# Global attention and a convolutional layer in one kernel: the values of 29 blocks as seven block products each

## The chip, the core and the metric

The kernel runs on one core of a Trainium2 chip. The metric is the device time of one execution in microseconds (us), the median of several runs. The core has five engines with queues of their own: TensorE (PE in the profile; its weight loads are shown apart as PEld), VectorE (DVE), ScalarE (ACT), GpSimd (POOL) and SyncE (SP), which here issues most DMA transfers. [...] All data is float32. Each float32 matmul of the kernel shows as two instructions in the trace.

## What is computed

The input is four images of 64 x 64 pixels with 256 channels. The first layer is global self-attention, and the second a perception convolution, a two-layer network on each pixel, and local 3 x 3 attention. Cut to what matters:

```python
# layer 0, per image: N = 4096 pixels, C = 256 channels
q = x @ Wq + bq                      # 32 columns
k = x @ Wk + bk
v = x @ Wv + bv                      # 256 x 256: the part that is changed
attn = softmax(q @ k.T)
x = gamma * (attn @ v) + x
# layer 1
perceived = depthwise_3x3(x, w_perc) # 3 outputs per channel
hid = gelu(perceived @ w_up1 + b_up1)
h = x + hid @ w_up2 + b_up2
out = h + local_attention_3x3(h, w_qkv, b_qkv)
```

## The kernel before

**Blocks and slots.** An image is cut into 8 blocks of 512 pixels (8 rows). Four images give 32 blocks, and the main loop has one slot for each: `for slot in range(NSLOT)`. In slot s, the global attention of block s runs against all pixels of its image. Behind it, with fixed lags, run the layers that follow, for earlier blocks: the convolution of block s-2 (`perceive`), the network of block s-3 (`hidden_part`, `update_part`, `guide_part`) and the local attention of block s-5.

**Points.** A slot has 16 points, `point = 2 * G + half`, where G is the key block of 512 pixels and half its first or second 256 pixels. At an even point `energy` makes the scores of the next key block (4 PSUM banks, tile e); at every point `weight` takes their exponentials on ScalarE (tile p), the jobs in `jobs[point]` follow, then `product` adds values times weights into two banks (tile acc), and `add_up` adds the weights on VectorE for the denominator (tile den). Then VectorE gets as many steps of the convolution as `share[point]` says: 6, 7, 7, 5, 4, 3, 3, 3, 2, 2, 4, 5, 5, 4, 0, 0. A step is a tap of 512 elements (line 477) or a mix of two quarters of 256 (line 483). At a slot's end `partial_sums` and `finish` divide the sums, add to the pixels, and release acc. All this is a schedule written by hand (`tc.manual_schedule`): the program order is each engine's queue order, and the framework adds the waits that data and buffers require.

**Banks.** PSUM is held by e (4 banks, one buffer), acc (2) and tag "m" (2 buffers). Every other product of the main loop, `job_bank(name)` or `bank("m", name)`, takes the next "m" bank in turn, and waits until the use before last of it has been read out.

**Values.** `project_v(s, pair)` makes the values of 256 pixels of block s: two tiles of 128 pixels, each two matmuls (256 input channels in two halves) of 256 columns, into one bank, and one ScalarE copy into tile v. `staged[s]` (tile xc and others) holds the block's pixels, channels on partitions, in two channel halves; `project_qk(s)` makes queries and keys of blocks s and s+1 out of them. Tile v has 8 buffers, one image. Blocks 0 to 2 are done ahead of the loop and blocks 3 to 7 in slot 0 (`early_jobs`). The values of the next image, in slots 7, 15 and 23 (`g == NBLK - 1`), come in `nxt[G]` behind the product and the convolution steps of each odd point: both halves of one block, and at every other one a `project_qk`. `fetch` loads the pixels two blocks ahead.

**Seven products.** Other products of the kernel are already made as seven block products instead of eight (Winograd's form of Strassen's algorithm): `hidden_part`, `update_part`, `guide_part`. `mix_weights` on GpSimd makes four mixes t1 to t4 of a weight's four blocks, VectorE makes mixes of the moving side, the products are called a to g and come in the parts "ab", "cd", "eg", "f", and `gather` puts each part's sums together: one ScalarE copy and one VectorE sum for ab, two sums for cd, three for eg, one for f. A part is read out by the sums that stand in VectorE's queue at that place. In `update_part` and `guide_part` the parts stand in points of their own, or two parts in one point.

Of the kernel before, what the change touches and what calls it, by code (L numbers as in the profile page):

```python
# [9 lines left out]
F32 = mybir.dt.float32  # L10
AF = mybir.ActivationFunctionType
ALU = mybir.AluOpType
# [40 lines left out]
def attention_then_perception_kernel(  # L53
# [37 lines left out]
    def unshifted():  # L91
# [184 lines left out]
                values[s][:, 2 * pair : 2 * pair + 2, :], ps.rearrange("p (t c) -> p t c", c=C)  # L276
            )

        def projections(s):
            pair = [lambda: project_qk(s)] if s % 2 == 0 else []  # L280
            return [lambda: project_v(s, 0), lambda: project_v(s, 1)] + pair

        def spread_queries(s):

# [227 lines left out]
        lower = by_turns(range(NPC), range(LOW, TAPS), RB - 1, RB)  # L512


        wmix = pool.tile([P, 4, MULT, C], F32, tag="wmix", name="wmix")


        wmix2 = pool.tile([P, 3, CH, P], F32, tag="wmix2", name="wmix2")
# [2 lines left out]
        def mix_weights(y11, y12, y21, y22, t1, t2, t3, t4):  # L521
            for to, a, b in ((t1, y12, y11), (t2, y22, t1), (t3, y22, y12), (t4, y21, t2)):
                nc.gpsimd.tensor_tensor(to, a, b, ALU.subtract)
# [42 lines left out]
        def hidden_part(s, d, part):  # L566


            if d == 0 and part == 0:
                hids[s] = tile_of([P, NHC, NB], "hid", f"hid_{s}")  # L570

            q = hids[s].rearrange("p d (a n) -> p (d a) n", a=2)
            q11, q21, q12, q22 = 2 * d, 2 * d + 1, 2 * d + 4, 2 * d + 5
            y11, y21 = (lambda j, u=u: wup1[:, u + j, bass.ts(d, P)] for u in (0, MULT))
            y22 = lambda j: wup1[:, MULT + j, bass.ts(d + 2, P)]
            t1, t2, t3, t4 = (lambda j, i=i: wmix[:, i, j, bass.ts(d, P)] for i in range(4))

            def products(name, *todo):
                ps = job_bank(f"hid_{s}_{d}_{name}")
                for n, (w, kind) in enumerate(todo):  # L580
                    for j in range(MULT):
                        nc.tensor.matmul(  # L582
                            ps[:, n * C : (n + 1) * C], lhsT=w(j), rhs=mixes[s, j][:, kind, :],
                            start=(j == 0), stop=(j == MULT - 1),
                        )
                return ps.rearrange("p (a n) -> p a n", a=2)

            def add(to, a, b):
                nc.vector.tensor_tensor(to, a, b, ALU.add)  # L589

            def twice(t):
                return t.unsqueeze(1).to_broadcast([P, 2, C])

            if part == 0:
                nc.scalar.copy(q[:, q22, :], products("a", (y11, LOWER))[:, 0, :])
                bc = products("bc", (y21, UPPER), (t2, MIX2))
                add(q[:, q11 : q22 + 1 : q22 - q11, :], bc, twice(q[:, q22, :]))
            else:
                de = products("de", (t3, MIX3), (t1, MIX1))
                both = q[:, q21 : q12 + 1 : q12 - q21, :]  # L600
                add(both, de, twice(q[:, q22, :]))
                add(q[:, q22, :], q[:, q21, :], de[:, 1, :])
                add(both, products("gf", (t4, UPPER2), (y22, MIX4)), both)
                for i in (d, d + 2):
                    nc.scalar.activation(  # L605
                        hids[s][:, i, :], hids[s][:, i, :], AF.Gelu, bias=bup1[:, i : i + 1]
                    )
# [411 lines left out]
        def local_product(s, c, behind=None):  # L1019
# [30 lines left out]
            nc.vector.tensor_tensor(rv, ov, pixels(s, c), ALU.add)  # L1050
            nc.sync.dma_start(out=out[b, :, c, bass.ts(g, NB)], in_=res)

        def job(f, s, *args, n=NSLOT):
            return [lambda: f(s, *args)] if 0 <= s < n else []

# [24 lines left out]
        def early(s):  # L1080
            fetch(s)
            fetch(s + 1)
            project_qk(s)

        early_jobs = [lambda: early(4), *projections(3), lambda: early(6)]
        early_jobs += [*projections(4)[:2], *projections(5), *projections(6)[:2], *projections(7)]
        points = 2 * NG
        for slot in range(NSLOT):
            b, g = divmod(slot, NBLK)
            if slot >= RING:  # L1090
# [13 lines left out]
            ]  # L1104
            if slot in (1, 2):
                jobs[0] = [lambda: next(combine)] * 2
            nxt = []
            if g == NBLK - 1 and b + 1 < B:
                nxt = [projections(slot + 1 + i) for i in range(NBLK)]
                for i in range(2):  # L1110
                    fetch(slot + 1 + i)
            if slot == 0:
                nxt = [early_jobs[2 * i : 2 * i + 2] for i in range(NG)]
            conv = perceive(slot - LAG_PERC, mixed) if slot >= LAG_PERC else iter(())
            n_mixed = NPC * (TAPS - 1) + MULT * len(MIXED)
            n_steps, stepped = n_mixed, 0
# [3 lines left out]
            if slot == NSLOT - 1:  # L1120

                nc.sync.dma_start(out=wup2[:, :CH, P:], in_=w_up2[:, :CH, P:])


                jobs = [
                    job(hidden_part, k, 0, 0) + job(local_values, k - 1, 1),
                    job(local_denominator, a) + job(hidden_part, k, 0, 1),
                    job(hidden_part, k, 1, 0), job(hidden_part, k, 1, 1) + job(local_product, a, 0),
                    job(update, k, 0), job(update, k, 1) + job(local_product, a, 1),
                    job(guide, k, 0) + job(local_values, k, 0),  # L1130
                    job(guide, k, 1) + job(local_values, k, 1),
                    job(scores, k, 0) + job(hidden_part, k + 1, 0, 0),
                    job(scores, k, 1) + job(local_sum, k - 1) + job(hidden_part, k + 1, 0, 1),
                    job(hidden_part, k + 1, 1, 0) + job(local_total, a + 1)
                    + job(local_reciprocal, a + 1),
                    job(hidden_part, k + 1, 1, 1), job(update, k + 1, 0) + job(border, k),
                    job(local_product, a + 1, 0) + job(update, k + 1, 1),
                    job(local_product, a + 1, 1) + job(local_values, k + 1, 0),
                    job(local_values, k + 1, 1),
                ]  # L1140
                conv = chain(conv, perceive(slot - 1, upper))
                n_steps += NPC * (TAPS - 1)
            for point in range(points):
                G, half = divmod(point, 2)
                after = slot + (G + 1) // NG, (G + 1) % NG
                if half == 0:
                    if G == NG // 2 and slot + 1 < NSLOT:
                        spread_queries(slot + 1)
                    if after[0] < NSLOT:
                        energy(*after)  # L1150
                if after[0] < NSLOT:
                    weight(*after, half)
                for do in jobs[point]:
                    do()
                product(slot, G, half)

                if point == 0:
                    add_up(slot, 0, 0)
                if point < points - 1:
                    add_up(slot, *divmod(point + 1, 2))  # L1160
                else:
                    partial_sums(slot)


                if slot < NSLOT - 1:
                    to = sum(share[: point + 1])
                else:
                    to = min(n_steps, -(-(point + 1) * n_steps // (points - 2)))
                    if point < 3:
                        to = min(to, n_mixed // MULT)  # L1170
                while stepped < to:
                    next(conv, None)
                    stepped += 1
                if slot == 0 and point == NG:

                    next(combine)
                    blqk = loaded(b_lqk, "blqk")
                    wperc = loaded(w_perc, "wperc")
                    bperc = loaded(b_perc, "bperc")
                    wup1 = loaded(w_up1, "wup1")  # L1180
                    bup1 = loaded(b_up1, "bup1")
                    wup2 = loaded(w_up2, "wup2")
                    mix_weights(
                        *blocks_of(wup1, MULT, C), *(wmix[:, i] for i in range(4))
                    )
                    y = blocks_of(wup2, CH, P)
                    mix_weights(*y, wmix2[:, 0], wmix2[:, 1], y[1], wmix2[:, 2])
                    bup2 = loaded(b_up2, "bup2")
                    nc.sync.dma_start(out=wlv, in_=w_qkv[:, :, 2 * C :])
                    blv = loaded(b_lv.partition_broadcast(P), "blv", [P, C])  # L1190
                if nxt and half == 1:
                    for do in nxt[G]:
                        do()
                    if slot and G + 2 < NBLK:
                        fetch(slot + 1 + G + 2)
            for _ in conv:
                pass
            if slot < NSLOT - 1:
# [467 lines left out]
```

## Time and profile before

| | |
|---|---|
| median of 3 runs | 3459.62 us (3457.77 to 3460.63) |
| profiled span | 3455.9 us |
| TensorE clock granted | 0.999 |
| slot 7 / slot 8 | 137.15 us / 102.05 us |
| values, line 270 | 512 matmul instructions, 116.3 us of TensorE |
| copies of values, line 275 | 64 on ScalarE, 586 ns each |
| attention product, line 323 | 4096 instructions, 1835.0 us of TensorE |

A line of the profile's groups reads: source line, engine, operation, output <- inputs, shapes and count | busy time in us, mean ns of one | idle time of the engine just before, and what ended it. Matmuls are pipelined, so the mean of one is longer than the step from one to the next; busy time counts overlaps once. The chain of waits is the chain of work that ended last, followed back from the end; where it stays on one engine without gaps, that engine's work is the time.

### The profile page before, as it was taken

Reading aid. Unit: us, or ns where it says so; the run is one execution under the profiler, and the core shown is the slowest. Engines: PE = TensorE matmul, PEld = TensorE weight load, DVE = VectorE, ACT = ScalarE, POOL = GpSimd, SP = SyncE. Lnnn points to the kernel's source line nnn. Section 1 sums busy time; section 2 is a strip of 40 time slices with the busy share of each in tenths; the row PEclk is TensorE's granted clock in tenths of the full one; section 3 lists DMA queues with packets and bytes.
Section 4 is the critical chain, followed back from the end, with each engine's and each line's share of the span. In section 5 each row is a group of like instructions: output and inputs, shape, how many; then the busy total and the mean of one; then the engine's idle time right before and its main releaser. Section 6 shows DMA issues by size and latency. Waiting matters only on the chain.

```text
span 3455.9 us, 33709 instructions
## 1 busy us (share of the span) xinstructions
PE 3442.0 (100%) x12726; PEld 1995.0 (58%) x12726; DVE 2736.2 (79%) x4439; ACT 1063.8 (31%) x1328; POOL 355.7 (10%) x525
## 2 busy tenths in 40 slices
PE   9999999999999999999999999999999999999998
PEld 5445555556555556556555555566656555555555
DVE  2388888767888888875888888887688888888885
ACT  3233333323332233333333323333233333223331
POOL 2000001110111110111001111101110011111021
PEclk9999999999999999999999999999999999999999
DMA  4000000120000000011000000001100000000000
GB/s 107 7 4 10 7 10 16 28 48 17 16 15 8 16 16 16 22 28 43 16 10 16 10 13 16 16 22 30 41 16 16 16 10 7 16 16 18 7 7 26
DMA packets 93274, 67.05 MB, mean 19 GB/s; under 512 B 65872, under 2 KB 71248, under 8 KB 92976
## 3 DMA queue, kind: packets, MB, share of 16 engines
q1 hardware_dynamic: 92432, 64.42, 6.9%
q8 instruction: 102, 1.67, 0.2%
q14 instruction: 68, 0.56, 0.1%
q10 hardware_dynamic: 672, 0.39, 0.0%
HBM read 43.62 MB, written 18.81 MB: 18 GB/s over the span
## 4 chain that ended last, share of the span: by engine, by line
PE 98%; DVE 1%; DMA 0%; SPq 0%; ACT 0%; issue 0%; ACTq 0%; POOL 0%; DVEq 0%
PE acc L323 51%; PE e L304 8%; PE hid_de L582 4%; PE hid_gf L582 4%; PE hid_bc L582 4%; PE v L270 3%; PE lv L891 3%; PE lo L1025 3%; PE s L932 3%; PE hid_a L582 3%; PE dx_ab L534 2%; PE dx_cd L534 1%; PE dx_eg L534 1%; PE hid L614 1%; PE g_cd L534 1%; PE qk L236 1%
## 5 line engine op out<-in xcount | busy, mean ns | idle before, releaser
L323 PE MATMUL acc<-p,v 128*128 128x512 f32 x4096 | 1835.0, 594 | 0.3 <-DVE o L388 0.3
L323 PEld LDWEIGHTS acc<-p,v 128*128 128x128 f32 x4096 | 768.0, 190 | 809.9 <-issue 793.0
L477 DVE SCALAR_TENSOR_TENSOR perc<-xp,wperc,perc 128x512 f32<-128x512 f32 (+2 forms) x1554 | 1101.2, 770 | 32.4 <-ACT perc L473 32.2
L312 ACT ACTIVATE p<-e 128x1024 f32<-128x1024 f32 x512 | 524.0, 1024 | 1717.5 <-PE e L304 713.3
L337 DVE TENSOR_TENSOR den<-den,p 128x1024 f32<-128x1024 f32 x480 | 586.4, 1222 | 86.5 <-ACT p L312 84.7
L957 POOL TENSOR_TENSOR lp<-lp,near 128x396 f32<-128x396 f32 x60 | 96.4, 1607 | 2490.8 <-ACT lp L952 2490.8
L304 PE MATMUL e<-qa,ka 32*128 32x512 f32 x2048 | 291.9, 640 | 0.0
L304 PEld LDWEIGHTS e<-qa,ka 32*128 32x128 f32 x2048 | 80.0, 182 | 166.2 <-issue 145.2
L582 PE MATMUL hid_de<-perc,wmix 128*128 128x256 f32 x720 | 165.2, 379 | 0.0
L582 PEld LDWEIGHTS hid_de<-perc,wmix 128*128 128x128 f32 x720 | 136.8, 190 | 43.7 <-issue 21.5
L483 DVE TENSOR_TENSOR perc<-perc 128x256 f32<-128x256 f32 x360 | 153.5, 440 | 8.2
L605 ACT ACTIVATE hid<-hid,bup 128x512 f32<-128x512 f32 x120 | 80.1, 714 | 219.4 <-DVE hid L589 219.4
L473 ACT ACTIVATE perc<-xp,bperc,wperc 128x512 f32<-128x512 f32 x192 | 145.3, 805 | 0.0
L980 POOL TENSOR_TENSOR lsum<-lsum,lp 128x99 f32<-128x99 f32 x168 | 122.3, 735 | 11.0
L1025 PEld LDWEIGHTS lo<-lp,lv 128*128 128x128 f32 x732 | 102.9, 191 | 35.1 <-issue 27.3
L891 PE MATMUL lv<-wlv,h 128*128 128x256 f32 x520 | 122.4, 379 | 0.0
L589 DVE TENSOR_TENSOR hid<-hid_bc,hid 128x512 f32<-128x512 f32 x60 | 41.5, 692 | 101.9 <-PE hid_bc L582 101.9
L270 PE MATMUL v<-wv,xc 128*128 128x256 f32 x512 | 116.3, 380 | 0.2 <-DMA wv<-in_w_v 0.2
L270 PEld LDWEIGHTS v<-wv,xc 128*128 128x128 f32 x512 | 97.0, 190 | 28.2 <-issue 15.2
L932 PEld LDWEIGHTS s<-lq,h 128*128 128x128 f32 x520 | 87.1, 188 | 37.3 <-issue 27.4
L891 PEld LDWEIGHTS lv<-wlv,h 128*128 128x128 f32 x520 | 98.7, 190 | 15.5 <-issue 2.2
L1025 PE MATMUL lo<-lp,lv 128*128 128x99 f32 (+1 forms) x732 | 107.4, 295 | 0.0
(194 smaller groups left out, 3102.5 us busy)
## 6 DMA issues: line engine op xcount, KB each, us to landing
xp<-in_x SPq DMA_DIRECT2D x30, 528.0 KB, 4.1
xc<-in_x SPq DMA_DIRECT2D x56, 256.0 KB, 3.7
out<-lo SPq DMA_DIRECT2D x56, 256.0 KB, 2.0
qa<-packed SPq DMA_DIRECT2D x124, 64.0 KB, 2.1
out<-res SPq DMA_DIRECT2D x8, 256.0 KB, 2.0
ka<-st SPq DMA_DIRECT2D x124, 16.0 KB, 1.8
packed<-st SPq DMA_DIRECT2D x31, 64.0 KB, 1.9
wup<-in_w_up SPq DMA_DIRECT2D x1, 1536.0 KB, 6.6
```

Of the source, the lines that this page charges most:

```text
L270: nc.tensor.matmul(ps[:, i * C : (i + 1) * C], lhsT=xc[:, kin, bass.ts(2 * pair + i, P)], rhs=wv[:, kin, :], start=(kin == 0), stop=(kin = ...
L304: nc.tensor.matmul(e[:, j, :], lhsT=key[rows, :], rhs=queries[s][rows, :], start=True, stop=True,)
L312: nc.scalar.activation(p, energies[s, G][:, 2 * half : 2 * half + 2, :], AF.Exp)
L323: nc.tensor.matmul(accs[s][c], lhsT=v[:, 2 * half + i, bass.ts(c, P)], rhs=p[:, i, :], start=(first and i == 0), stop=(G == NG - 1 and hal ...
L337: nc.vector.tensor_tensor(den, den, p, ALU.add)
L477: nc.vector.scalar_tensor_tensor(acc, win, wt, acc, ALU.mult, ALU.add)
L483: nc.vector.tensor_tensor(t[:, to, :], t[:, a, :], t[:, b, :], op)
L534: nc.tensor.matmul(ps[:, n * C : (n + 1) * C], lhsT=w(j), rhs=values(j), start=(j == 0), stop=(j == kin - 1),)
L582: nc.tensor.matmul(ps[:, n * C : (n + 1) * C], lhsT=w(j), rhs=mixes[s, j][:, kind, :], start=(j == 0), stop=(j == MULT - 1),)
L891: nc.tensor.matmul(ps[:, half * C : (half + 1) * C], lhsT=keys_of(s, t, half, kin), rhs=wlv[:, kin, :], start=(kin == 0), stop=(kin == CH ...
L932: nc.tensor.matmul(ps[:, t * QR * QW : t * QR * QW + rows * QW].rearrange("p (h w) -> p h w", w=QW), lhsT=keys_of(s, t, half, kin), rhs=gu ...
L1025: nc.tensor.matmul(pv[:, rows, columns(half)], lhsT=lvs[block, t, half][:, bass.ts(c, P)], rhs=near_ws[block, half][:, t, of, :], start=(i ...
```

## The change

The values of blocks 3 to 31 are made as seven block products instead of eight: 512 pixels x 256 channels in, 256 out, cut in half along each of the three. The first three blocks stay as they were. `project_part(s, part)` takes the place of `project_v` for the 29 blocks:

- The pixels are the stationary side (128 x 128 tiles), and the weight blocks the moving side of 128 columns: 14 matmuls of 128 columns for a block in place of 8 of 256.
- The pixels' mixes are made in place in `staged[s]` by VectorE: b12 = b11 - b12, b11 = mix1 - b11, b21 = b21 - b11, with mix1 = b12 + b22 held in a quarter of the block's own value tile. The projection of queries and keys stands ahead of the mixes.
- `gather` sums the products into the tile v: seven sums on VectorE and one ScalarE copy, in place of two ScalarE copies.
- In slots 7, 15 and 23, part ab of block i (and project_qk for even i) stands ahead of the product of point 2(i+1), and cd, eg and f stand behind that product and that point's convolution steps; for the eighth block this is point 0 of the next slot. In slot 0 ab comes behind an odd point, and the rest behind the next odd point.
- `mix_weights` makes the mixes of wv, with t3 in place of its block y12. To the same end the third mix of w_up1 is now made in place (tile wmix has three parts, not four). Both plain blocks are loaded again in the last slot, for the blocks of the tail that use them plain and for the guarded second path.

The core of the diff:

```diff
+        def project_part(s, part):
+            if part == "ab":
+                v = tile_of([P, TPB, C], "v", f"v_{s}", NBLK)
...
+                nc.vector.tensor_tensor(mix1, b12, b22, ALU.add)
+                nc.vector.tensor_tensor(b12, b11, b12, ALU.subtract)
...
+            todo = dict(
+                ab=((b11, y11), (b21, y21)), cd=((b11, t2), (b12, y12)),
+                eg=((mix1, t1), (b22, t4)), f=((b21, y22),),
+            )[part]
+            ps = job_bank(f"v_{s}_{part}").rearrange("p (n j c) -> p n j c", j=2, c=P)
+            for n, (tokens, w) in enumerate(todo):
+                for j in range(2):
+                    nc.tensor.matmul(
+                        ps[:, n, j, :], lhsT=tokens[:, j, :], rhs=w, start=True, stop=True
+                    )
+            if part == "ab":
+                nc.vector.tensor_tensor(b11, mix1, b11, ALU.subtract)
+                nc.vector.tensor_tensor(b21, b21, b11, ALU.subtract)
+            gather(part, [ps[:, n] for n in range(len(todo))], *quarters, None)
+
+        def rest(s):
+            for part in ("cd", "eg", "f"):
+                project_part(s, part)
...
-        wmix = pool.tile([P, 4, MULT, C], F32, tag="wmix", name="wmix")
+        wmix = pool.tile([P, 3, MULT, C], F32, tag="wmix", name="wmix")
...
+        def plain_hidden():
+            nc.sync.dma_start(out=wup1[:, :MULT, C:], in_=w_up1[:, :MULT, C:])
...
-        early_jobs = [lambda: early(4), *projections(3), lambda: early(6)]
-        early_jobs += [*projections(4)[:2], *projections(5), *projections(6)[:2], *projections(7)]
+        y = [w[:, 0] for w in blocks_of(wv, 1, P)]
+        mix_weights(*y, vmix[:, 0], vmix[:, 1], y[1], vmix[:, 2])
+        early_jobs = [[lambda: early(4)], [lambda: early(6)], [], [], [], []]
+        for i in range(3, NBLK):
+            early_jobs[i - 3] += [lambda i=i: project_part(i, "ab")]
+            early_jobs[i - 2].insert(0, lambda i=i: rest(i))
...
-                nxt = [projections(slot + 1 + i) for i in range(NBLK)]
-                for i in range(2):
-                    fetch(slot + 1 + i)
+                for i in range(NBLK):
+                    s, at = slot + 1 + i, points * slot + 2 * (i + 1)
+                    ahead[at] = job(project_qk, s) if i % 2 == 0 else []
+                    ahead[at] += job(project_part, s, "ab")
+                    behind[at] = job(rest, s)
...
-                for do in jobs[point]:
+                at = points * slot + point
+                for do in jobs[point] + ahead.pop(at, []):
                     do()
                 product(slot, G, half)
...
-                if nxt and half == 1:
-                    for do in nxt[G]:
-                        do()
+                for do in behind.pop(at, []):
+                    do()
```

More of the change, by code (lines that the diff above doesn't have):

```diff
@@ L277, in project_v @@
             )
-        def projections(s):
-            pair = [lambda: project_qk(s)] if s % 2 == 0 else []
-            return [lambda: project_v(s, 0), lambda: project_v(s, 1)] + pair
+        vmix = pool.tile([P, 3, P], F32, tag="vmix", name="vmix")
+        value_mixes = {}
+        def project_part(s, part):
+            if part == "ab":
+                v = tile_of([P, TPB, C], "v", f"v_{s}", NBLK)
+                values[s] = v
+                quarters = [
+                    v[:, 2 * n : 2 * n + 2, bass.ts(c, P)] for n in range(2) for c in range(2)
+                ]
+                b11, b12, b21, b22 = (
+                    staged[s][:, kin, bass.ts(n, C)].rearrange("p (j n) -> p j n", n=P)
+                    for kin in range(2) for n in range(2)
+                )
+                mix1 = quarters[1]
+                value_mixes[s] = quarters, (b11, b12, b21, b22, mix1)
+                nc.vector.tensor_tensor(mix1, b12, b22, ALU.add)
+                nc.vector.tensor_tensor(b12, b11, b12, ALU.subtract)
+            quarters, (b11, b12, b21, b22, mix1) = value_mixes[s]
+            y11, y12, y21, y22 = (y[:, 0] for y in blocks_of(wv, 1, P))
+            t1, t2, t4 = (vmix[:, i] for i in range(3))
+            todo = dict(
[7 more added lines that the diff above has]
+                        ps[:, n, j, :], lhsT=tokens[:, j, :], rhs=w, start=True, stop=True
+                    )
+            if part == "ab":
[5 more added lines that the diff above has]
+                project_part(s, part)
         def spread_queries(s):
@@ L574, in hidden_part @@
             y11, y21 = (lambda j, u=u: wup1[:, u + j, bass.ts(d, P)] for u in (0, MULT))
-            y22 = lambda j: wup1[:, MULT + j, bass.ts(d + 2, P)]
-            t1, t2, t3, t4 = (lambda j, i=i: wmix[:, i, j, bass.ts(d, P)] for i in range(4))
+            t3, y22 = (lambda j, u=u: wup1[:, u + j, bass.ts(d + 2, P)] for u in (0, MULT))
+            t1, t2, t4 = (lambda j, i=i: wmix[:, i, j, bass.ts(d, P)] for i in range(3))
             def products(name, *todo):
@@ L1083, in early @@
             project_qk(s)
-        early_jobs = [lambda: early(4), *projections(3), lambda: early(6)]
-        early_jobs += [*projections(4)[:2], *projections(5), *projections(6)[:2], *projections(7)]
+        y = [w[:, 0] for w in blocks_of(wv, 1, P)]
[4 more added lines that the diff above has]
+            early_jobs[i - 2].insert(0, lambda i=i: rest(i))
         points = 2 * NG
+        ahead, behind = {}, {}
         for slot in range(NSLOT):
@@ L1106, in unshifted @@
                 jobs[0] = [lambda: next(combine)] * 2
-            nxt = []
             if g == NBLK - 1 and b + 1 < B:
-                nxt = [projections(slot + 1 + i) for i in range(NBLK)]
-                for i in range(2):
-                    fetch(slot + 1 + i)
+                for i in range(NBLK):
[3 more added lines that the diff above has]
+                    behind[at] = job(rest, s)
+                    if i < 2:
+                        fetch(s)
+                    if i + 2 < NBLK:
+                        behind[at] += job(fetch, s + 2)
             if slot == 0:
-                nxt = [early_jobs[2 * i : 2 * i + 2] for i in range(NG)]
+                behind = {2 * i + 1: todo for i, todo in enumerate(early_jobs)}
             conv = perceive(slot - LAG_PERC, mixed) if slot >= LAG_PERC else iter(())
@@ L1122, in unshifted @@
                 nc.sync.dma_start(out=wup2[:, :CH, P:], in_=w_up2[:, :CH, P:])
+                nc.sync.dma_start(out=wv[:, 0, P:], in_=w_v[:, 0, P:])
                 jobs = [
@@ L1135, in unshifted @@
                     + job(local_reciprocal, a + 1),
-                    job(hidden_part, k + 1, 1, 1), job(update, k + 1, 0) + job(border, k),
+                    job(hidden_part, k + 1, 1, 1) + [plain_hidden],
+                    job(update, k + 1, 0) + job(border, k),
                     job(local_product, a + 1, 0) + job(update, k + 1, 1),
@@ L1182, in unshifted @@
                     wup2 = loaded(w_up2, "wup2")
[L1183 to L1187, printed above, removed]
+                    for y, mix in ((blocks_of(wup1, MULT, C), wmix), (blocks_of(wup2, CH, P), wmix2)):
+                        mix_weights(*y, mix[:, 0], mix[:, 1], y[1], mix[:, 2])
                     bup2 = loaded(b_up2, "bup2")
@@ L1190, in unshifted @@
                     blv = loaded(b_lv.partition_broadcast(P), "blv", [P, C])
-                if nxt and half == 1:
-                    for do in nxt[G]:
-                        do()
-                    if slot and G + 2 < NBLK:
-                        fetch(slot + 1 + G + 2)
+                for do in behind.pop(at, []):
+                    do()
             for _ in conv:
```

## The prediction

> **What bounds the kernel now.** I read the engine shares of the page first, then the chain of waits, then the costliest groups.
>
> ```profile
> PE 3442.0 (100%) x12726; PEld 1995.0 (58%) x12726; DVE 2736.2 (79%) x4439; ACT 1063.8 (31%) x1328; POOL 355.7 (10%) x525
> PE 98%; DVE 1%; DMA 0%; SPq 0%; ACT 0%; issue 0%; ACTq 0%; POOL 0%; DVEq 0%
> ...
> L270 PE MATMUL v<-wv,xc 128*128 128x256 f32 x512 | 116.3, 380 | 0.2 <-DMA wv<-in_w_v 0.2
> ```
>
> TensorE is the chain: 98% of it, with hardly any gap. So whatever TensorE is spared comes off the time, and whatever it is made to wait goes on. The line of the values has 512 instructions for 32 blocks, 16 each. VectorE has 21% free on average; what counts is how much it has where the values are made. The stage table (busy time of each engine in stretches) answers for slot 7, which makes all values of the second image, and slot 8:
>
> ```profile
> 647.30:784.45 137.15, 137.15 (x542) 85.58 (x542) 87.44 (x140) 43.27 (x59) 9.14 (x13) 1.00 0.20 45
> 784.45:886.50 102.05, 102.05 (x382) 59.31 (x382) 86.91 (x140) 32.12 (x40) 10.88 (x14) 1.00 0.05 14
> ```
>
> The columns are length, then busy time of PE, PEld, DVE, ACT, POOL. Slot 7 is 35.1 us longer, which is eight values and four query/key projections (8 x 3.45 + 4 x 1.87) in the chain in order of time. VectorE does the same 87 us in both, and rests in slot 7 while values are made:
>
> ```profile
> 699.99 3.46 PE acc L323 x8
> 703.45 3.45 PE v L270 x16
> 706.90 1.87 PE qk L236 x8
> 708.77 1.07 PE e L304 x8
> ...
> 826.84 1.54 PE lo L1025 x12
> ```
>
> A block's values cost 3.45/16 = 216 ns an instruction of 256 columns; a product of attention with values costs 3.43 us.
>
> [...] lo has 12 instructions in 1.54 us, four of 198 columns at 167 ns (s: eight in 1.34), so the eight of 99 columns take 109 ns each and not the 83 of their width. [...] in slot 7 VectorE's instructions come in program order. [...] 4 for e, 2 for acc, 2 under "m". So a third job in a row must wait for the first one's bank. Where the kernel already does this (g_ab, lv, g_cd in point 9), the timeline shows it:
>
> ```profile
> 852.77 0.48 DVE L548 SCALAR_TENSOR_TENSOR lq<-g_ab,small,lq 128x256 f32<-128x256 f32 x1
> 853.30 0.73 PEld L534 LDWEIGHTS g_cd<-gmix,gmix 128*128 128x128 f32 x4 [0.39 <-DVE lq L548]
> ```
>
> g_cd waits for VectorE to empty g_ab's bank; its four instructions take 1.12 us in the chain, not the 0.86 of four others. I take 0.25 us from the emptying to full flow, and bound it by 0.1 and 0.3.
>
> **The change, part by part.**
>
> *TensorE work.* 16 instructions of 256 columns become 28 of 128 columns. 128 columns stream in 107 ns (half of 216) [...], so 28 x 0.108 = 3.02 us against 3.45: 0.43 us saved a block, 12.5 us for 29. High bound: 0.112 each, which leaves 0.31.
>
> *ScalarE* loses two copies of 586 ns and gets one of 370: nothing, at 31% busy.
>
> *VectorE* gets four mixes and seven sums of 256 elements at 0.42 to 0.45 us (the row of h<-dx_eg, three in 1.34): about 4.8 us a block, 38 us in slot 7. 87 + 38 = 125 is below the 134 us that TensorE would need, so the sum alone fits. The order decides.
>
> *Order.* Before, the values came after an odd point's product, emptied by ScalarE. Now ab stands ahead of the even product; cd, eg and f come behind it. In VectorE's queue, cd's sums stand behind the mixes of b11 and b21 (which cannot start until the first ab product is done, 0.43 us before the attention product P starts), q11's sum, the add-up of the next weights (step 1.14), and the point's taps (0.674 each; seven in 4.72) or block mixes (0.42). f takes cd's bank, so TensorE stands until cd's sums are done, and behind f stands everything else, with no slack.
>
> Counted from P = 0, TensorE is ready for f at 3.43 + 0.86 + 0.86 = 5.15. If VectorE is free in time, q11 is done at 0.86, the add-up at 2.00, then the taps; cd's sums (0.88) start then, or at 4.32 at the earliest; f starts 0.25 after them. By slot 7's points:
>
> - point 2: three taps, four mixes, 3.70: sums at 5.70, f at 6.83, wait 1.68
> - point 4: four taps, 2.70; VectorE comes 1.82 late from point 3's taps, lo's sums and the two mixes: f at 7.64, wait 2.49
> - point 6: three taps: f at 5.45, wait 0.30
> - point 8: after dx_f come 0.42 + 1.65 + 1.6 us of bias and `guide_mix` and our 0.88, while TensorE has only ab: VectorE is 4.14 late. cd waits 1.00 for b11, f 1.96
> - point 10: qk waits 1.27 for g_eg's bank, f 0.67 (four taps)
> - point 12: five taps, 1.35
> - point 14: no taps, 0.30
> - point 0 of slot 8: six taps, the first copy 0.66, and VectorE 1.17 late from the last block's closing sums: f at 9.00, wait 3.85
>
> Waits for f: 12.6. The job after f needs eg's bank, whose three sums (1.34) follow cd's: it waits 1.34 + 0.25 against 0.25 + 0.43 of f, some 0.9, after six of the eight blocks (after points 12 and 14 no such job comes): 5.3. With 1.00, 1.27 and 0.7 for the denominator at the slot's end: 20.9. Saved: 8 x 0.43 = 3.4. Net +17.4 for each of slots 7, 15 and 23, which have the same jobs: **+52**. Done the same way for slot 7 of the kernel before, the sum gives 137.2 us where the trace has 137.15.
>
> *Slot 0* (five blocks): no taps, VectorE 25 us busy of 105. f waits 0.3 for cd's sums, and the next job 0.9 in four of five: +5.1, saved 2.2. Some 0.9 hides in a wait for xc that a projection has anyway (2.80 us instead of 1.87). **+2**.
>
> *The rest.* Mixing wv on GpSimd (four subtractions of 128x128) falls in slot 0, where it is mostly idle. wmix has the same subtractions, one in place. The two reloads in the last slot land long before they are read: the profile lands the whole w_up of 1536 KB in 6.6 us, and hid needs it some 40 us later. Releasing xc later: the last pair's pixels are fetched behind f of point 12 and read by qk of point 14, 4.8 us later, against 3.7 us to landing: nothing, at most 1 us an image. No effect on the tail.
>
> Sum: 3459.6 + 52 + 2 = **3514 us**.
>
> **Rivals.**
>
> *All saved.* VectorE runs ahead, banks come free in time: 3459.6 - 12.5 = 3447. For it: slots 7 and 8 show long VectorE rests (7.3 us before point 2's hid_bc). Against: the mixes of b11 and b21 tie VectorE to TensorE at every block, the taps lie between, and there is no third bank.
>
> *Break-even.* Waits of 3.4 an image change, if most taps were done before P: 3460. Against: only where a point has no taps (14) or few (6) are the waits that small.
>
> *VectorE becomes the bound.* It falls behind for good: backlog from points 4, 8 and 0 reaches the late points' gelu and exponentials, and slots 7, 15, 23 lengthen by 30 or more: 3459.6 + 90 + 5 = 3555. For it: 125 us of work in 134. Against: points 9 to 15 give it room, as the waits themselves do.
>
> **How the numbers follow.** Forecast 0.83, all saved 0.09, break-even 0.04, VectorE the bound 0.04. Within the forecast: the least is point by point without lateness and with 0.1 us to flow, +11 an image change and 0 in slot 0, 3493; the most is 22 and 6 us, with the xc wait, 3532. Some slack below for waits that overlap: 3488 to 3532. Faster by over 0.2% (under 3452.7): 0.09. Within 0.2%: 0.04. Slower: 0.87.
>
> **What would show it.** Right: TensorE idle, some 50 us in all, before v_f and the job after it, put down to VectorE's sums of v_cd and v_eg; slot 7 near 147 us and slot 8 near 110 (the eighth block's products and waits now fall in it), and so at 15 and 23; v instructions spaced 108 ns; VectorE's busy share up by some 4 points. Wrong: v_f following v_eg without a gap, or v instructions spaced by much more than 110 ns (190, the length of a load's record, would alone cost 1.9 us a block, 54 in all, in the wrong place).

## The result, and the profile after

The changed kernel takes 3535.91 us (median of 4 runs, 3533.86 to 3537.86) against 3458.69 us for the kernel before: ratio 1.0223, 95% interval 1.0205 to 1.0240, so 77 us slower. The forecast was 3514 us, slower by 54, with a range of 3488 to 3532 that misses the measured time by 4 us.

First the engine shares and the chain of waits on the page of the changed kernel:

```profile
PE 3463.2 (98%) x13074; PEld 2013.7 (57%) x13074; DVE 2859.4 (81%) x4758; ACT 1040.6 (29%) x1299; POOL 357.2 (10%) x529
PE 92%; DVE 6%; issue 1%; SPq 0%; ACT 0%; DMA 0%; DVEq 0%; POOL 0%; ACTq 0%; POOLq 0%
```

Before, TensorE was 98% of the chain and VectorE 1%. Now VectorE is 6% of it: the chain leaves TensorE where TensorE stands and waits. That VectorE's busy share rose only from 79 to 81% (the forecast had some 4 points) says little, since its new work is in seven slots of 32, slot 0 among them, and the span grew with it. The stage table for slots 7 and 8 (length, then busy time of PE, PEld, DVE, ACT, POOL; the third number from the end is the granted clock, the share of TensorE's full clock that the trace shows as granted) tells more:

```profile
651.29:801.80 150.51, 136.85 (x610) 84.89 (x610) 116.62 (x217) 36.98 (x50) 9.41 (x13) 0.99 0.18 41
801.80:913.30 111.50, 107.30 (x410) 63.79 (x410) 91.22 (x151) 32.02 (x40) 10.90 (x14) 0.98 0.04 12
```

Slot 7 was 137.15 us long and TensorE busy in all of it; now it is 150.5 (forecast near 147), and TensorE stands for 13.7 us of it. Slot 8, which takes over the eighth block's last products, went from 102.05 to 111.5 (forecast near 110). Added up from the end of one slot to the next: slot 0 +4.0, slots 7 and 8 +22.8, 15 and 16 +25.3, 23 and 24 +25.3, all others the same to 0.2 us, and the last one with what follows it 0.4 us less. That is the 77.

The chain in order of time, at slot 7's point 2, shows how it comes about:

```profile
677.24 0.66 PE v_ab L309 x4
677.92 0.44 DVE xc L313
...
678.45 0.42 DVE xc L314
678.87 0.34 DVE v L585
679.21 1.13 DVE den L375
680.34 2.00 DVE perc L515 x3
682.36 0.44 DVE perc L521
682.82 0.77 DVE perc L521 x2
683.61 0.42 DVE perc L521
684.03 0.35 DVE v L585
684.40 0.77 DVE v L585 x2
...
686.22 4.51 PE hid_de L621 x12
690.74 2.60 PE hid_gf L621 x12
```

From ab the chain goes over to VectorE, whose instructions come here in the order of the program: two mixes of the pixels, the first sum of the values, the add-up of the weights, three taps, four block mixes, and only then the sums of cd and eg, behind which TensorE takes up hid_de, a part of the hidden layer's product. The attention product lies hidden in these 8 us. The last two lines show a second thing: hid_de and hid_gf are twelve instructions of 256 columns each, yet the first takes 4.51 us and the second 2.60. The stage table of the first gives a granted clock of 0.62:

```profile
686.20:690.74 4.54, 4.52 (x13) 3.72 (x14) 0.21 (x1) 0.00 (x0) 0.00 (x0) 0.62 0.58 119
```

The waits of TensorE, summed (engine, waiting line, what ended it: us in total, times, longest):

```profile
PE v_f L309 <- DVE v L585: 37.6, 29, 3.6
PE hid_de L621 <- DVE v L585: 3.4, 6, 0.6
PE qk L236 <- DVE lq L587: 3.4, 3, 1.1
PE v_cd L309 <- DVE xc L313: 2.1, 3, 0.7
PE v_ab L309 <- DVE v L585: 2.0, 3, 0.7
```

v_f waits in all of its 29 blocks, and for VectorE's line 585, the sums in `gather`.

### The profile page after: what moved, and what is told of

Same layout as the page of the kernel before. It is cut to its first block, busy times and chain, and to the rows that moved or that the text cites. A ratio compares the mean times of both kernels' runs of the same rounds, so it can differ in the third digit from the quotient of the medians.

```text
span 3532.9 us, 34837 instructions
## 1 busy us (share of the span) xinstructions
PE 3463.2 (98%) x13074; PEld 2013.7 (57%) x13074; DVE 2859.4 (81%) x4758; ACT 1040.6 (29%) x1299; POOL 357.2 (10%) x529
## 4 chain that ended last, share of the span: by engine, by line
PE 92%; DVE 6%; issue 1%; SPq 0%; ACT 0%; DMA 0%; DVEq 0%; POOL 0%; ACTq 0%; POOLq 0%
PE acc L361 48%; PE e L342 8%; PE hid_de L621 5%; PE hid_gf L621 4%; PE hid_bc L621 4%; PE lv L930 3%; PE lo L1064 3%; PE s L971 3%; PE hid_a L621 3%; DVE perc L515 2%; DVE v L585 2%; PE dx_ab L573 2%; PE dx_cd L573 1%; PE dx_eg L573 1%; PE hid L653 1%; PE g_cd L573 1%
## 5 line engine op out<-in xcount | busy, mean ns | idle before, releaser
L930 PEld LDWEIGHTS lv<-wlv,h 128*128 128x128 f32 x520 | 100.0, 192 | 16.2 <-issue 2.2
L971 PE MATMUL s<-lq,h 128*128 128x198 f32 (+1 forms) x520 | 100.4, 334 | 2.1 <-DVE v L585 1.7
L621 PE MATMUL hid_de<-perc,wup 128*128 128x256 f32 x360 | 93.1, 397 | 3.4 <-DVE v L585 3.4
L621 PE MATMUL hid_a<-perc,wup 128*128 128x256 f32 x360 | 93.6, 396 | 0.0
```

What stands on the lines that cost most here:

```text
L621: nc.tensor.matmul(ps[:, n * C : (n + 1) * C], lhsT=w(j), rhs=mixes[s, j][:, kind, :], start=(j == 0), stop=(j == MULT - 1),)
L930: nc.tensor.matmul(ps[:, half * C : (half + 1) * C], lhsT=keys_of(s, t, half, kin), rhs=wlv[:, kin, :], start=(kin == 0), stop=(kin == CH ...
L971: nc.tensor.matmul(ps[:, t * QR * QW : t * QR * QW + rows * QW].rearrange("p (h w) -> p h w", w=QW), lhsT=keys_of(s, t, half, kin), rhs=gu ...
```

## The experiments

Two theories stood against each other, and a third cost had to be put apart. **Theory:** TensorE waits for a PSUM bank which VectorE empties only behind the point's taps; the order of VectorE's queue is what costs. **Rival:** VectorE has too much work in slots 7, 15 and 23, whatever its order. **Third:** the products of 128 columns are slow in themselves.

### Only slot 0 changed

```diff
...
-                    ahead[at] = job(project_qk, s) if i % 2 == 0 else []
-                    ahead[at] += job(project_part, s, "ab")
-                    behind[at] = job(rest, s)
+                    behind[at - 1] = job(project_v, s, 0) + job(project_v, s, 1)
+                    behind[at - 1] += job(project_qk, s) if i % 2 == 0 else []
...
```

> Seven products for the five blocks of slot 0 alone; the values of slots 7, 15 and 23 are made as before, eight products behind the odd points (wv keeps all four plain blocks, its third mix has a tile of its own). Theory (the cost is TensorE waiting where VectorE has the convolution's taps in its queue, so at the image changes): slot 0 stays 4.0 us longer, everything else is as before, 3459 + 4 = 3463 us. Rival (the in-place mix of w_up1, the reloads or the clock cost time everywhere): well above 3470 us. Rival (the 128-column products are slow in themselves): slot 0 pays 5/29 of 77 us, 3472 us.

Measured: 3461.06 us against 3458.55, ratio 1.0007 (0.9998 to 1.0016). The interval takes in 1, so the trace has to tell: slot 0 takes 114.9 us, 4.1 more than before, and every other slot its time of before to 0.2 us. Only behind the last slot are there 2.8 us more, a stretch of half clock that this execution has and the profiled one of the kernel before has not (it was the slowest of the twelve). So the in-place mix of w_up1 and the reloads cost nothing that shows, and the loss is at the image changes.

### The price of 128 columns, by itself

```diff
-                for kin in range(CH):
+                for c in range(CH if s > 2 else 0):
+                    for kin in range(CH):
+                        nc.tensor.matmul(
+                            ps[:, i * C + c * P : i * C + (c + 1) * P],
+                            lhsT=xc[:, kin, bass.ts(2 * pair + i, P)],
+                            rhs=wv[:, kin, bass.ts(c, P)],
...
+                for kin in range(CH if s <= 2 else 0):
                     nc.tensor.matmul(
                         ps[:, i * C : (i + 1) * C],
...
```

> The kernel before, with each 256-column matmul of the values of blocks 3 to 31 cut into two of 128 columns with a weight load each: 32 instructions a block instead of 16, nothing else. Theory (a 128-column instruction costs 112 ns, as between the changed kernel's own products): 32 x 0.112 - 3.45 = +0.13 us a block, 29 blocks, 3463 us. Rival (a weight load costs the 190 ns of its record when it can't hide): 32 x 0.19 - 3.45 = +2.6 us a block, 3535 us.

Measured: 3461.50 us, ratio 1.0008 (0.9999 to 1.0017), 2.95 us more for 29 blocks, 0.10 a block: (3.45 + 0.10)/32 = 111 ns an instruction. The interval takes in 1, but the trace agrees: slots 7, 15 and 23 are each 0.9 us longer for eight blocks, and the instructions of a block start 0.112 us apart. Its groups (busy time, mean ns of one) show 928 such instructions in 108.6 us, with the overlap of the last one of each block counted in, though the record of each reads 275 ns:

```profile
L271 PE MATMUL v<-wv,xc 128*128 128x128 f32 x928 | 108.6, 275 | 0.0
```

The third cost is out. The changed kernel's own products keep the same step: v_cd's two halves start at 681.60 and 682.04, four instructions in 0.44 us.

### ScalarE reads the banks, VectorE sums later

```diff
+            outs = [ps[:, n] for n in range(len(todo))]
+            if part == "cd":
+                both = staged[s][:, 0, :].rearrange("p (n j c) -> p n j c", j=2, c=P)
+                nc.scalar.copy(both, ps)
+                outs = [both[:, n] for n in range(2)]
+            elif part == "eg":
+                spare_v = tile_of([P, 2, P], "read", f"read_{s}")
+                nc.scalar.copy(b22, outs[0])
+                nc.scalar.copy(spare_v, outs[1])
+                outs = [b22, spare_v]
+            elif part == "f":
+                nc.scalar.copy(b21, outs[0])
+                outs = [b21]
-            gather(part, [ps[:, n] for n in range(len(todo))], *quarters, None)
+            gather(part, outs, *quarters, None)
```

> The changed kernel, but cd, eg and f are read out of their banks by ScalarE copies, into the block's own pixels (dead by then) and one small tile; VectorE makes the same seven sums from there, at the same place of its queue. VectorE's work is unchanged, only the banks no longer wait for its taps. Theory (TensorE waits for the bank that VectorE empties behind its taps): no wait before f, 0.4 us instead of 0.8 before the next job, the waits for b11 at point 8 (0.9) and for qk at point 10 (1.3) stay, the granted clock stays at 1.0: +5 us an image change, up to +8 if the pixels, which are released later, hold up the next fetch: 3459 + 3 x (5 to 8) = 3474 to 3483 us. Rival (VectorE simply has too much work in slots 7, 15 and 23): no better than the changed kernel, 3530 us or more.

Measured: 3486.01 us, ratio 1.0079 (1.0062 to 1.0096): 50 of the 77 us are gone, with all of VectorE's sums still there (it is busy 2862.4 us, against 2859.4). No wait before v_f is left in the list of TensorE's waits. Of its first four lines, the first two are larger than above; the other two are as above:

```profile
PE qk L236 <- DMA xc<-in_x: 6.0, 5, 1.3
PE dps L427 <- DVE parts L409: 4.4, 3, 1.5
PE qk L236 <- DVE lq L600: 3.4, 3, 1.1
PE v_cd L309 <- DVE xc L313: 2.1, 3, 0.7
```

The first is the one that I had put at up to 3 us an image change: the pixels are released later. In slots 15 and 23 it costs 1.1 to 1.3 us each. In slot 7 the projection of point 14 stands for pixels twice, 1.2 us each, and a stretch of half clock comes behind, from 779.2 to 782.6 us, so that this image change takes 2.9 us more than the two others. The second line, the wait for the denominator, was not in my list at all. hid_de, which no long wait precedes any more, is back at 2.6 us. So the theory holds for the bulk, and the rival, VectorE's mere load, does not. Not all of the 50 us are waits: the half-clock stretches in the image changes fall from 34.1 us to 3.4.

### VectorE's sums ahead of its taps

```diff
                 product(slot, G, half)
+                if slot:
+                    for do in behind.pop(at, []):
+                        do()

                 if point == 0:
...
```

> The changed kernel, but in slots 7, 8, 15, 16, 23, 24 the sums of cd, eg and f stand ahead of the add-up and the taps of the point in VectorE's queue; TensorE's order is unchanged. Theory: f waits only 0.3 us everywhere, the job after f still some 0.85; VectorE now rests for 3.4 us of each even product and is late in other places (point 6's update by 2 us, point 14's border by 3, the slot's end by 2): net +14 us an image change, 3459 + 3 x 14 + 4 = 3505 us, with few clock drops. Rival (too much VectorE work): no better than 3536 us. Rival (taps are not what f waits for): the wait before f stays at 1 to 4 us.

Measured: 3511.42 us, ratio 1.0150 (1.0133 to 1.0167). The wait before f falls to 0.2 us in each of 28 blocks, now that no tap stands ahead of cd's sums. The gain is 24.5 us and not more because VectorE now rests through the product and is late at the slot's end (dps, the product for the denominator) and at the border (c):

```profile
PE dps L414 <- DVE parts L396: 6.9, 3, 2.3
PE c L914 <- DVE edge L903: 5.3, 3, 1.8
PE v_f L309 <- DVE v L585: 4.9, 28, 0.2
PE v_ab L309 <- DVE h L585: 4.3, 3, 1.4
```

A change of order alone, no operation more or less, moves the time by 24 us. It was 6 us longer than expected: an image change costs 16.2 to 17.7 us and not the 14 expected, and clock drops are part of it (hid_a took 2.72 us instead of 1.40 behind the wait for the denominator; there are four half-clock stretches of 3.4 us in the image changes).

### A ladder of made waits

The half-speed hid_de was not in the forecast. To see what brings it about, TensorE was made to wait in slots of the kernel before that have nothing to do with the change:

```diff
+        def hold(slot):
+            n = 2 + 4 * (slot - 8 if slot < 16 else slot - 16) + (2 if slot < 16 else 0)
+            ps = job_bank(f"hold_{slot}")
+            nc.tensor.matmul(ps[:, :16], lhsT=ones, rhs=ones[:, :16], start=True, stop=True)
+            nc.vector.tensor_copy(step, ps[:, :16])
+            for _ in range(n):
+                nc.vector.tensor_tensor(step, step, step, ALU.max)
+            nc.tensor.matmul(ps[:, 16:32], lhsT=ones, rhs=step, start=True, stop=True)
...
```

> The kernel before, with a made wait in point 15 of slots 8 to 14 and 16 to 22: a tiny matmul, a chain of 2 to 28 VectorE operations of 16 elements that reads it, and a tiny matmul that reads the chain's end; TensorE stands in between for some 0.5 to 6 us, a different time in each slot, and then goes on with the attention product. Theory (the half-speed hid_de of the changed kernel comes from TensorE's idle time just before it): after waits under 1 us all eight instructions of the product keep their step of 429 ns; after waits of 4 us and more the first ones take near twice that (858 ns) for about 3 us, 1.5 to 2 us lost; between 1.5 and 4 us some do and some don't. Rival (the clock has to do with hid_de, or with the values' products): every product keeps its step.

Measured, in one execution, from the timeline of each slot: TensorE's idle time between the two tiny products, and what the eight instructions of the attention product behind them took (3.5 us at full clock). From the start of the first tiny product to that of the attention product it is 0.5 to 0.75 us more, in which TensorE has next to nothing to do either.

| idle before, us | 0.68 | 1.10 | 1.52 | 1.94 | 2.35 | 2.77 | 3.19 | 3.61 | 4.03 | 4.45 | 4.87 | 5.28 | 5.70 | 6.12 |
|---|---|---|---|---|---|---|---|---|---|---|---|---|---|---|
| product took, us | 3.5 | 3.5 | 3.5 | 3.5 | 5.2 | 6.3 | 3.5 | 6.2 | 5.2 | 5.8 | 5.4 | 5.2 | 6.5 | 6.2 |

Up to 1.94 us nothing is lost. From 2.35 us on, 9 of 10 waits cost another 1.7 to 3.0 us, and one (3.19) nothing. One step of the ladder in the timeline:

```profile
1091.58 0.29 PE L1094 MATMUL hold<-ones 128*128 128x16 f32 x2
1094.64 0.61 PE L1098 MATMUL hold<-step,ones 128*128 128x16 f32 x2 [2.77 <-DVE step L1097]
1095.09 6.48 PE L324 MATMUL acc<-p,v 128*128 128x512 f32 x8
1101.41 0.30 PE L377 MATMUL dps<-parts,fold 128*128 128x32 f32 x2
```

The product has nothing to do with values or hid_de, so it is the idle time. In the changed kernel the losses are of the same size, and shorter waits close together do it too: 1.4 and 0.6 us before hid_de at point 2 of slot 7, though not at the same point of slots 15 and 23.

Where the half clock (0.50 granted) begins is not mere chance. In the clock record of the changed kernel's trace, all half-clock stretches but the one at the very end are 3.41 us long or twice that (six and two of them), and start whole multiples of 3.41 us apart (at 686.55, 819.67, 1580.84 us and so on: 39 and then 223 times 3.41). So that trace can be cut at such multiples into pieces of 3.41 us, with every one of these stretches beginning at a cut. The ladder's trace is cut here from the half-clock stretch that begins at 1988.21 us; 2090.61 and 2094.03 lie 30 and 31 times 3.41 us behind it. The stage table of such pieces, for the waits of 2.35 and 3.19 us (columns as above):

```profile
1984.80:1988.21 3.41, 1.06 (x6) 0.60 (x4) 2.97 (x14) 1.02 (x1) 0.00 (x0) 1.00 0.00 0
1988.21:1991.63 3.42, 3.42 (x6) 1.55 (x6) 2.34 (x4) 0.17 (x1) 0.25 (x1) 0.50 0.00 0
2090.61:2094.03 3.42, 1.86 (x7) 0.80 (x5) 3.15 (x11) 1.02 (x1) 0.20 (x1) 1.00 0.00 0
2094.03:2097.44 3.41, 1.78 (x6) 1.07 (x7) 3.06 (x11) 0.17 (x1) 0.00 (x0) 1.00 0.00 0
```

The wait of 2.35 us lies in one piece, which leaves TensorE busy for 1.06 us of it, and the next piece has half clock. The longer wait of 3.19 us is split by the cut between two pieces, 1.86 and 1.78 us busy, and costs nothing. At point 2 of slot 7 of the changed kernel both short waits fall into one piece (busy 1.41 us of 683.14 to 686.55), and in slot 15 a cut at 1560.36 us parts them (busy 1.98 us of the piece before it). At what busy share the clock drops is not settled: in the changed kernel's trace, from 41 to 3523 us, TensorE is busy for 0.68 to 1.44 us of the eight pieces of full clock that half clock follows, and for 1.94 us or more of those that full clock follows; in the ladder 1.78 us cost nothing.

### All banks freed

With e2's reading, the products of a block stand in the order f, cd, eg, and ab and the query/key projection move behind the odd product:

```diff
         def rest(s):
-            for part in ("cd", "eg", "f"):
+            for part in ("f", "cd", "eg"):
                 project_part(s, part)
...
-                    ahead[at] = job(project_qk, s) if i % 2 == 0 else []
-                    ahead[at] += job(project_part, s, "ab")
+                    odd = behind.setdefault(at - 1, [])
+                    odd += job(project_qk, s) if i % 2 == 0 else []
+                    odd += job(project_part, s, "ab")
...
```

> The seven products for 29 blocks, with every wait I know of taken away: ScalarE reads out cd, eg and f as before; the products' order is f, cd, eg, so that each bank is empty when it comes up again; ab and the query/key projection stand behind the odd product, where the values stood in the kernel before. Theory: waits left per image change: 1 us at g_cd, 1.2 for the denominator at the slot's end, 1 in the next slot's first jobs, 3.5 us, against 8 x 0.32 us of saved products and a wait of 0.3 that goes: +0.4; slot 0 gains 1.6: 3459 + 1 - 2 = 3458 us, no clock drops. Rival (VectorE's 38 us more in the slot set the time): 3480 us or more.

Measured: 3484.64 us, ratio 1.0074 (1.0061 to 1.0088), 27 us more than expected and, by the time alone, a win for the rival. The list of waits says otherwise: the largest is for a transfer.

```profile
PE qk L236 <- DMA xc<-in_x: 12.6, 8, 3.4
PE dps L436 <- DVE parts L418: 3.2, 3, 1.1
PE hid_a L643 <- DVE v L607: 1.9, 3, 0.6
```

I had overlooked it: the eighth block's pixels take the sixth's buffer, and the projection that reads them now comes one point after the sums that release it. It waits 3.1 to 3.4 us for them at each image change, with half clock behind it at two of the three.

### The sums moved on a point

Against the run before:

```diff
...
-                    later = behind[at]
+                    later = behind[at] if i == NBLK - 2 else behind.setdefault(at + 1, [])
                     later += job(sum_up, s)
...
```

> As the run with all banks freed, and each block's six sums of cd, eg and f on VectorE move on behind the next odd point's taps (but for the seventh block of an image, whose pixels' buffer is needed at once). Theory: VectorE's work no longer comes in one lump ahead of point 9's g_cd and of the slot's end: waits left 1.9 us an image change, net -1.2; slot 0 -1.6: 3459 - 3.6 - 1.6 = 3454 us, the first version below the kernel before. Rival: the same as the run without the move or slower, since VectorE is late at other points.

Measured: 3551.12 us, ratio 1.0266 (1.0252 to 1.0281), slower than all. It is the same oversight made worse, since the pixels are released a point later still: TensorE waits 58.2 us for them in all, 8.1 at most. What the move does to VectorE is hidden under that.

```profile
PE qk L236 <- DMA xc<-in_x: 58.2, 11, 8.1
```

### The pixels freed as well

Against the run with all banks freed:

```diff
+        def room(s, kin):
+            if s >= NBLK and s % NBLK == 5:
+                return hids[s - 6 - LAG_HID][:, kin, :]
+            return staged[s][:, kin, :]
...
-                both = staged[s][:, 0, :].rearrange("p (n j c) -> p n j c", j=2, c=P)
+                both = room(s, 0).rearrange("p (n j c) -> p n j c", j=2, c=P)
...
```

> As the run with all banks freed, but for the sixth block of each image, whose products ScalarE copies into the hidden layer's tile (unused from point 9 to the slot's end) and not into the block's pixels, so that the load of the eighth block's pixels starts when TensorE is done with them, and not when VectorE's sums are. Theory (what that run lost against its forecast is the wait of 3.2 us for those pixels in point 13, and clock drops after it): 3.4 to 4.5 us less an image change, 3485 - 3 x 4 = 3473 us. Rival (VectorE's load in the slot, or ScalarE's copies): 3482 us or more.

Measured: 3471.42 us, ratio 1.0030 (1.0019 to 1.0042). 13 us are gone, as expected, with VectorE's and ScalarE's work unchanged. Slot 7 takes 137.0 us, as before, and slot 8 106.7, 4.6 more; slots 15 and 16 the same, 23 and 24 1.7 us less, without a clock drop. Some 3 us more, in the profiled execution, are again half clock behind the last slot. The seven products now cost little, but they still bring nothing. In slots 7 and 8 the largest remainders are 1.1 us for the denominator, 0.6 us before hid_a, a clock drop in hid_a behind these two (2.7 us instead of 1.4), 1.7 us at one projection (3.56 instead of 1.87, 0.6 of it a wait for pixels), and 0.1 to 0.2 us at each ab (0.99 to 1.09 us instead of 0.89). None of the versions beats the kernel before.

## Why the prediction was right and wrong

**Right: the waits, and their size before f.** TensorE stands before f for cd's bank, which VectorE empties behind its taps. Point by point, in the first image change, the gap between eg's last step and f's first, against the forecast's own list:

| point | 2 | 4 | 6 | 8 | 10 | 12 | 14 | 0 of slot 8 | sum |
|---|---|---|---|---|---|---|---|---|---|
| forecast, us | 1.68 | 2.49 | 0.30 | 1.96 | 0.67 | 1.35 | 0.30 | 3.85 | 12.6 |
| measured, us | 1.60 | 2.40 | 0.34 | 1.79 | 0.55 | 2.76 | 0.35 | 3.81 | 13.6 |

The job after f: forecast 5.3, measured 4.9 (0.8 to 0.9 in each of the six blocks). cd at point 8: 1.00 and 0.86. qk at point 10: 1.27 and 1.29. The denominator: 0.7 and 0.5. Two runs show that order and banks, and not load, are behind it: 50 us go when ScalarE reads the banks and 24 when the sums come first, with VectorE's sums kept in both (and the half clock that followed the waits goes with them).

**Wrong: the waits were taken as their own whole cost.** The step that failed is "whatever it is made to wait goes on": the forecast added each wait at its own length and put what follows it at nothing, without a reason. Half-clock stretches behind the waits cost 3.5 us in slots 7 and 8 (hid_de twice 1.75 us over its 2.6). In 15 and 16, and again in 23 and 24, they cost 6.1, in the products that then came up: lo 1.6, the attention product behind it 1.3, g_ab 1.0, lv 0.5, hid_de 1.7. Together 15.7 us, of a miss of 23. The clock record agrees: it has 34.1 us of half clock in these six slots, so at most half of that, 17.1 us, was lost. The ladder shows how short a wait can do it: 2.35 us of idle were enough where they fell into one piece of 3.41 us, and TensorE was busy for 1.06 us of that piece. The forecast itself had waits of 2.5 and 3.85 us in its list and didn't ask what TensorE would do after them.

**Wrong: point 12.** Its five taps were priced at 0.674 each, from a stretch in which GpSimd rests. There they take 4.38 us, while `local_sum` runs on GpSimd; the mix just before takes 0.99 us instead of 0.42:

```profile
775.63 0.99 DVE L314 TENSOR_TENSOR xc<-xc 128x256 f32<-128x256 f32 x1
...
776.88 5.74 POOL L1019 TENSOR_TENSOR lsum<-lsum,lp 128x99 f32<-128x99 f32 x6
778.01 4.38 DVE L515 SCALAR_TENSOR_TENSOR perc<-xp,wperc,perc 128x512 f32<-128x512 f32 x5
```

The wait before f was 1.4 us longer than forecast, 4.2 us over three image changes. The trace of the kernel before shows the same over the whole run: of its 1518 taps of 512 elements, the 1355 that overlap no instruction of GpSimd have records of 0.73 to 0.75 us, and the 163 that do have 1.04 on average and 1.45 at most. So the price could have been read beforehand. That GpSimd is the cause is still only suggested; no run takes its work away.

**Smaller terms.** A 128-column instruction takes 111 to 112 ns, not 108 (half of the 216 ns of one with 256 columns): 28 x 0.0037 x 29 = 3.0 us. That lay within the bounds given, whose upper end was 112. Slot 0 costs 4.0 us instead of 2: f and the next job waited as forecast. Of the rest, 0.8 us lies at the slot's start (the first attention product comes 0.4 us later, and the first projection waits 0.76 us for its pixels instead of 0.32), and the products of the five blocks save some 0.7 us less than forecast, most of which the 3.0 us already have.

15.7 + 4.2 + 3.0 + 2.0 = 24.9 us, against a miss of 77.2 - 54.3 = 22.9; the other terms were some 2 us too high together.

**The rivals.** "All saved" and "break-even" fell with the first list of waits: v_f waited in every block. "VectorE becomes the bound" didn't come either. It would have left slots 7, 15 and 23 at VectorE's own length, but VectorE is busy 116.6 us of slot 7's 150.5, and with the pixels freed the same sums fit into the 137.0 us of slot 7 (117.2 us busy). The range was too narrow: its upper end allowed for larger waits, but not for a cost behind them.

## What to carry to other kernels

A saving on a full TensorE is worth what is left after the waits that its new order brings: before adding a job to a point, count the banks in use, and look up what stands in the emptying engine's queue ahead of the instruction that empties the third one. Where TensorE would stand as long as it did here (2.35 us and more in the ladder, 1.4 and 0.6 us close together in slot 7), look for half clock behind it: in these traces 1.7 us were lost for each 3.41 us of it that were full of work, and one or two such stretches followed the waits of the ladder. And when an operand's buffer becomes scratch, follow its next load to the reader: two of the runs lost there what they had gained elsewhere.

## What was not expected of the hardware

- The clock drop behind waits of 2.35 us and more, 1.7 to 3.0 us each, in 9 of 10 such waits of the ladder; none in 4 waits up to 1.94 us. In the changed kernel's trace its stretches start only whole multiples of 3.41 us apart, and the one wait of the ladder that cost nothing (3.19 us) lay across a cut at such a multiple, 2094.03 us.
- VectorE's taps took up to twice as long (1.45 us instead of 0.74, and 1.04 on average in 163 taps) while GpSimd worked; shown side by side in time, not by an experiment.
